# Bringing a vector to every partition: four transposes of a repeated column in place of a product of ones with a diagonal

## The chip, the cores and the metric

One Trainium2 chip, one core of it. The metric is the device time of one execution in microseconds (us), median of several runs. Everything is computed in FP32.

## The reference

Two layers over 4096 nodes with 512 features each; `adj` is a 4096 x 4096 matrix of weights.

```python
# layer 0: attention, its scores shifted twice by adj
q = x @ Wq.T + bq;  k = x @ Wk.T + bk;  v = x @ Wv.T + bv
a = q @ k.T / sqrt(512) + adj + adj
x = layernorm(x + softmax(a, axis=-1) @ v)
# layer 1: two graph convolutions
h = relu(adj @ (x @ W1) + b1)            # 128 features
x = layernorm(x + adj @ (h @ W2) + b2)
```

## The kernel before, in words

q and k are never formed. With M = Wq^T Wk, the scores are x M x^T plus terms that depend on one of the two nodes only: a column vector g made of Wq and bk, a vector ub made of Wk and bq, and a constant c0 made of bq and bk. The scores are halved and computed transposed, keys on the 128 partitions and queries along the free axis, because `adj` enters twice and the exponential is taken with scale 2. The products of the scores, of the softmax with x, and of the layers' matrices are done by Strassen's scheme with seven products in place of eight.

Queries are worked on in 8 groups g of 512 (`W`), keys in 8 blocks d of 512. One step of a group takes two of the seven products' places; a pair of 128-row key tiles is a unit. The order of all engines' work is written out by hand: the tile framework's scheduler is off, `at(unit, n, f)` puts a function at a place n of a unit, and a list `work` gives the TensorE work that is spread between the score products (products of the softmax with x for the group before, its output rows, the next layer's projection). Each engine carries out its own instructions in that order.

Five small vectors are needed in a form in which every partition holds the whole vector along its free axis (128 x 512), though they come as columns (128 x 4, entry r*128 + p at partition p, column r):

- bk and bq, at the very start. They are multiplied with the rows of Wq^T and Wk^T by VectorE (`times`) to make g and ub, and with each other to make c0.
- g, which VectorE multiplies with the rows of x (`row_parts`) to get each query's constant c.
- c of a group (8 times): `add_c0(g)` adds c0, `row_consts(g)` makes the tile CB[g], with which `begin_scores` fills a tile of scores on ScalarE (line 380). A DMA on GpSimd's queue then adds `adj` to it (line 385).
- m, the maximum of each query of a group (8 times): `turn_max(g)` turns the running maximum by four transposes (line 468), reduces it on VectorE (line 474) to a column per 128 queries; `spread_max(g)` makes MB[g], which VectorE subtracts from the scores (`shift`, line 484) ahead of the exponential.

Before the change each of these is done in two steps. `spread` (line 397, VectorE) multiplies an identity with the column, which gives four 128 x 128 diagonals in one 128 x 512 tile; the tile lies in the pool `sap` of eight buffers, which also holds the left operands of the score products ("sa"). `in_every_row` (line 408, TensorE) multiplies a matrix of ones, which is a 128 x 1 column read repeatedly, with the diagonals: each sum over the partitions has one term that isn't zero. ScalarE copies the result from PSUM (line 411). In the profile one such FP32 product shows as two matmul records. For c and m the two steps stand at different places of the schedule: m is reduced at place 5 of unit s1 and spread at place 1 of unit s1 + 1, c is completed at place 1 and spread at place 3 of a unit.

The stage at the start, before the loop: load bk and bq (ScalarE's queue), Wq^T and Wk^T in two halves each, then x^T and x (SP's queue); spread bk and bq; transpose Wq^T (tile `wq_t` into `wq_n`) and Wk^T by 16 transposes of 128 x 128 each (line 855), copied out in turn by ScalarE and VectorE; `times` for g; M by 16 products of 128 x 512 (tile psm, line 864), with g's broadcast after the second group of four; the first u = M^T x^T (psu, line 262), with the first group's c after its first four products.

PSUM is used in banks: four for the tag "o" (weights, u, softmax products), one each for "x" and "y" (scores), and one each for "m0" and "m1", which alternate for broadcasts, turns and output rows.

Of the kernel before, what the change touches and what calls it, by code (L numbers as in the profile page):

```python
# [11 lines left out]
F32 = mybir.dt.float32  # L12
AF = mybir.ActivationFunctionType
ALU = mybir.AluOpType
# [4 lines left out]
P = 128  # L19
# [5 lines left out]
def tile_graph_attention_then_gcn(  # L25
# [51 lines left out]
    nc = tc.nc  # L77
# [8 lines left out]
    PER = W // P  # L86
# [5 lines left out]
    const = ctx.enter_context(tc.tile_pool(name="const", bufs=1))  # L92
# [1 line left out]
    psum = ctx.enter_context(tc.tile_pool(name="psum", bufs=2, space=PSUM))  # L94

    ident = const.tile([P, P], F32, name="ident")
    ones = const.tile([P, 1], F32, name="ones")
    half_t = const.tile([P, 1], F32, name="half_t")
    bq_t = const.tile([P, ND], F32, name="bq_t")
    bk_t = const.tile([P, ND], F32, name="bk_t")  # L100
    b1_t = const.tile([P, 2], F32, name="b1_t")
    t_sb = const.tile([P, NT, H], F32, name="t_sb")
    c_sb = const.tile([P, NT], F32, name="c_sb")
# [18 lines left out]
    sap = att.enter_context(tc.tile_pool(name="sap", bufs=8, side="right"))  # L122
# [8 lines left out]
    g_t = mp.tile([P, D], F32, name="g_t")  # L131
# [4 lines left out]
    def bank(tag, name, bufs=1):  # L136
        return psum.tile([P, W], F32, tag=tag, name=name, bufs=bufs)
# [3 lines left out]
    def mbank(name):  # L141

        m_tags.append(m_tags.pop(0))
        return bank(m_tags[-1], name)
# [13 lines left out]
    UT, UO, XTS, SA, S, XN, CB, MB, MACC, LACC, O, OT, RL, XR, T = ({} for _ in range(15))  # L158


    def load_xts(b):
        XTS[b] = xtp.tile([P, ND, W], F32, tag="xt", name=f"xt{b}")
        nc.sync.dma_start(XTS[b], xT[:, ts(b, W)].rearrange("(c p) i -> p c i", p=P))
# [227 lines left out]
    def pair(g, q):  # L391
        return S[g, q // 2][:, :, q % 2]

    def spread(col, name):

        dg = sap.tile([P, PER, P], F32, tag="sa", name=f"diag{name}")
        nc.vector.tensor_tensor(
            dg,
            ident.unsqueeze(1).to_broadcast([P, PER, P]),
            col.unsqueeze(2).to_broadcast([P, PER, P]),  # L400
            ALU.mult,
        )
        T["diag", name] = dg

    def in_every_row(name, into):
        dg = T.pop(("diag", name))
        ps = mbank(f"bc{name}")
        nc.tensor.matmul(
            ps, ones.to_broadcast([P, P]), dg.rearrange("p r i -> p (r i)"), start=True, stop=True
        )  # L410
        nc.scalar.copy(into, ps)  # L411

    def load_rows(g):
# [3 lines left out]
    def row_parts(i, xr):  # L417

        product = t_sb[:, 24 : 24 + PER, :].rearrange("p a b -> p (a b)")
        nc.vector.scalar_tensor_tensor(  # L420
            product, xr, 1.0, g_t, ALU.mult, ALU.mult, accum_out=c_sb[:, i : i + 1]
        )

    def add_c0(g):
        c = c_sb[:, ts(g, PER)]
        nc.vector.tensor_scalar(c, c, c0_t, None, ALU.add)
        spread(c, f"c{g}")

    def row_consts(g):
        CB[g] = bcp.tile([P, W], F32, tag="cb", name=f"cb{g}")  # L430
        in_every_row(f"c{g}", CB[g])


    def qk(g, d, k, j):
# [30 lines left out]
    def turn(acc, name):  # L465
        ps = mbank(name)
        for r in range(PER):
            nc.tensor.transpose(ps[:, ts(r, P)], acc[:, ts(r, P)], ident)
        return ps.rearrange("p (r j) -> p r j", j=P)

    def turn_max(g):
        ps = turn(MACC[g], f"mt{g}")
        m = small.tile([P, PER], F32, tag="m", name=f"m{g}")
        nc.vector.tensor_reduce(m, ps, AX.X, ALU.max)
        spread(m, f"m{g}")

    def spread_max(g):
        MB[g] = bcp.tile([P, W], F32, tag="mb", name=f"mb{g}")
        in_every_row(f"m{g}", MB[g])


    def shift(g, q, h):
# [315 lines left out]
    with tc.tile_pool(name="wqk", bufs=1) as wp:  # L798
        wk_t = wp.tile([P, ND, D], F32, name="wk_t")
        wq_t = wp.tile([P, ND, D], F32, name="wq_t")  # L800
        wk_n = wp.tile([P, ND, D], F32, name="wk_n")
        wq_n = wp.tile([P, ND, D], F32, name="wq_n")
        bq_r = wp.tile([P, W], F32, name="bq_r")
        bk_r = wp.tile([P, W], F32, name="bk_r")
        g_c = wp.tile([P, ND], F32, name="g_c")

        nc.scalar.dma_start(bk_t, bk)
        nc.scalar.dma_start(bq_t, bq)
        for w_t, wT in ((wq_t, wqT), (wk_t, wkT)):
            for o in range(2):  # L810
                nc.sync.dma_start(
                    w_t[:, :, ts(o, D // 2)],
                    wT.rearrange("(c p) o -> p c o", p=P)[:, :, ts(o, D // 2)],
                )
        make_identity(nc, ident)
        nc.gpsimd.memset(ones, 1.0)
        nc.gpsimd.memset(half_t, -0.5)
        load_xts(0)
        rows0 = t_sb[:, : PER * PER, :].rearrange("p (r a) b -> p r (a b)", r=PER)
        nc.sync.dma_start(rows0, x[:W, :].rearrange("(r p) d -> p r d", p=P))  # L820
        load_xts(1)
        for i in range(4):
            nc.gpsimd.dma_start(
                b1_t[ts(i // 2, H // 2), i % 2 : i % 2 + 1], b1[ts(i % 2, H // 2), :]
            )
        def evict(n, out_, in_):
            if n % 2:
                nc.vector.tensor_copy(out_, in_)
            else:
                nc.scalar.copy(out_, in_)  # L830

        def times(w_t, b_r, into):

            product = t_sb[:, 24 : 24 + PER, :].rearrange("p a b -> p (a b)")
            for c in range(into.shape[1]):
                nc.vector.scalar_tensor_tensor(
                    product,
                    w_t[:, c, :],
                    HALF_SCALE,
                    b_r,  # L840
                    ALU.mult,
                    ALU.mult,
                    accum_out=into[:, c : c + 1],
                )

        for name, b_t, b_r in (("bk", bk_t, bk_r), ("bq", bq_t, bq_r)):
            spread(b_t, name)
            in_every_row(name, b_r)


        for w_t, w_n in ((wq_t, wq_n), (wk_t, wk_n)):
            for o in range(ND):
                ps = bank("o", f"psw{o}", 4)
                for c in range(ND):
                    nc.tensor.transpose(ps[:, ts(c, P)], w_t[:, c, ts(o, P)], ident)
                evict(o, w_n[:, o, :], ps)
        times(wq_t, bk_r, g_c)
        spread(g_c, "g")
        times(wk_t, bq_r, ub_t)

        for a in range(ND):
            ps = bank("o", f"psm{a}", 4)
            for o in range(ND):
                nc.tensor.matmul(  # L864
                    ps, wq_n[:, o, ts(a, P)], wk_n[:, o, :], start=o == 0, stop=o == ND - 1
                )
            evict(a, m_t[:, a, :], ps)
            if a == 1:
                in_every_row("g", g_t)
                times(bq_r.unsqueeze(1), bk_r, c0_t)  # L870
                for r in range(PER):
                    row_parts(r, rows0[:, r, :])
                add_c0(0)
# [5 lines left out]
    for f in first[:ND]:  # L879
        f()  # L880
    row_consts(0)
    begin_scores(0, 0)
    add_scores(0, 0)
# [243 lines left out]
    for g in range(NG):  # L1127
        s0 = g * NP
        s1 = s0 + NP
        if g:  # L1130
            for n, k in enumerate(ORDER):
                at(s0 - 2 + (2 * n + 1) // 7, (2 * n + 1) % 7, load_operand, g, k)
            at(s0 - 2 - (g == 1), 1, add_c0, g)
            at(s0 - 2 - (g == 1), 3, row_consts, g)
        for q in range(NP):
# [12 lines left out]
            at(s1 + unit, n2, sums, g, q)  # L1148
            at(s1 + unit, n2, px_t2, g, q)
        at(s1, 5, turn_max, g)  # L1150
        at(s1 + 1, 1, spread_max, g)
        if g < NG - 1:
            at(s1 + 13, 4, row_sums, g)
# [25 lines left out]
    for unit in range(last_unit):  # L1179
# [30 lines left out]
        for n in range(len(ORDER)):  # L1210
            run(unit, n)
            g, place = divmod(unit * len(ORDER) + n, NP * len(ORDER))
# [10 lines left out]
            while todo and owed > 0.2:  # L1223
                us, f = todo.pop(0)
# [7 lines left out]
    g = NG - 1  # L1232
# [106 lines left out]
    for n, (i0, cols, ld) in enumerate(parts):  # L1339
        acc = bank("o", f"acce{n}", 4)[:, :cols]  # L1340
        per = 2048 // cols
        for j in range(NT):
# [4 lines left out]
            if j % (2, 5, 10, 20)[n] == (1, 3, 4, 6)[n]:  # L1347
# [5 lines left out]
                start=j == 0,  # L1353
                stop=j == NT - 1,
# [49 lines left out]
```

## Time and profile before

| What | Value |
|---|---|
| median of 3 runs | 2315.63 us (2314.59 to 2316.66) |
| the profiled execution's own time | 2315.36 us |
| its span | 2313.5 us |
| TensorE matmul (PE) busy | 2285.4 us |
| TensorE weight load (PEld) busy | 1750.6 us |
| VectorE (DVE) busy | 1636.5 us |
| GpSimd (POOL) busy | 1010.3 us |
| ScalarE (ACT) busy | 403.9 us |
| granted TensorE clock, mean | 0.999 |

How to read it: PE is TensorE's matmuls, PEld its weight loads, which overlap them. Matmuls overlap one another in the records and their ends are modelled, so the time that one holds TensorE is read from start to start. Rows in order of time give the start and duration in us, the engine, the line of the kernel, the operation, and output and inputs by their names in the program; "x4" is a merged row of four instructions, and brackets hold the idle time of the engine before it and what ended that. A line of waits reads: who waited, on whom, us in total, times, the longest. "The chain of work that ended last" follows the time back from the last instruction through whatever released each step.

TensorE's operations that the change touches, from the profile of before:

| Operation | Count | Recorded ns of one |
|---|---|---|
| ones times diagonal of c, of m (line 408), records | 16 and 16 | 592 |
| the same for bk, for bq, records | 2 and 2 | 1061 to 1192 |
| the same for g, records | 2 | 592 |
| diagonals on VectorE (line 397) | 19 | 691 to 695 |
| transposes of the maximum (line 468) | 32 | 272 to 329 |
| transposes of Wq, Wk (line 855) | 32 | 272 to 421 |
| ScalarE's copies behind a broadcast (line 411) | 19 | 585 |

### The profile page before, as it was taken

How to read it: one execution, taken by the hardware profiler on the slowest of the kernel's cores; microseconds unless marked ns; L12 is line 12 of the kernel's file. 1: busy time of each engine (PE TensorE's matmuls, PEld its weight loads, DVE VectorE, ACT ScalarE, POOL GpSimd, SP SyncE). 2: the span in 40 equal slices, each digit the busy share in tenths (PEclk: the TensorE clock that was granted, in tenths of full speed). 3: DMA queues.
4: the chain of work that ended last, by engine and by line, in shares of the span. 5: the costliest groups of instructions: out<-in, count | busy, mean ns of one | idle time of the engine just before them, and what ended most of it. 6: DMA issues, size and time to landing. Idle time of an engine off the chain costs nothing.

```text
span 2313.5 us, 28534 instructions
## 1 busy us (share of the span) xinstructions
PE 2285.4 (99%) x10662; PEld 1750.6 (76%) x10662; DVE 1636.5 (71%) x2295; ACT 403.9 (17%) x445; POOL 1010.3 (44%) x1010
## 2 busy tenths in 40 slices
PE   9999999999999999999999999999999999999998
PEld 5888788888888888888888888888876743333456
DVE  4676776686667766866776787668657877888864
ACT  2212211231122112111311221122102000000012
POOL 2566553184237424731653284237429830001043
PEclk9999999999999999999999999999999999999999
DMA  6899786667757684877577577847654468899996
GB/s 173 268 302 306 229 246 200 177 186 210 229 141 217 187 241 112 227 197 210 149 224 215 152 217 195 233 132 218 192 195 149 161 237 312 334 346 375 352 381 223
DMA packets 278008, 523.30 MB, mean 226 GB/s; under 512 B 19376, under 2 KB 126640, under 8 KB 276976
## 3 DMA queue, kind: packets, MB, share of 16 engines
q1 hardware_dynamic: 229040, 406.12, 52.1%
q0 software_dynamic: 43296, 105.39, 20.6%
q10 hardware_dynamic: 5536, 9.97, 1.2%
q8 instruction: 85, 1.39, 0.2%
q14 instruction: 51, 0.42, 0.0%
HBM read 473.44 MB, written 46.40 MB: 225 GB/s over the span
## 4 chain that ended last, share of the span: by engine, by line
PE 94%; DVE 3%; POOL 2%; issue 1%; ACT 0%; DMA 0%; POOLq 0%; DVEq 0%; ACTq 0%
PE p L581 32%; PE X L441 19%; PE b L1049 15%; PE Y L441 14%; PE psu L234 3%; PE v L708 3%; PE acce L1349 2%; PE ops L1303 1%; PE tps L754 1%; PE psu L262 1%; PE x L656 1%; PE x1ps L745 1%; DVE s L531 1%; PE psm L864 1%; DVE s L454 1%
## 5 line engine op out<-in xcount | busy, mean ns | idle before, releaser
L581 PE MATMUL p<-s,xn 128*128 128x256 f32 x3584 | 895.9, 380 | 6.7 <-DVE s L531 2.7
L581 PEld LDWEIGHTS p<-s,xn 128*128 128x128 f32 x3584 | 676.9, 190 | 111.4 <-DVE s L531 6.2
L441 PE MATMUL X<-ut,sa 128*128 128x256 f32 x1984 | 513.3, 381 | 1.6 <-DVE s L454 1.6
L497 POOL TENSOR_TENSOR lacc<-lacc,s 128x512 f32<-128x512 f32 x240 | 344.4, 1435 | 203.2 <-ACT s L488 192.3
L441 PEld LDWEIGHTS X<-ut,sa 128*128 128x128 f32 x1984 | 370.4, 190 | 67.4 <-DVE s L454 15.3
L454 DVE TENSOR_TENSOR s<-X,s 128x512 f32<-128x512 f32 x256 | 176.4, 689 | 272.8 <-PE X L441 272.4
L441 PE MATMUL Y<-ut,sa 128*128 128x256 f32 x1408 | 360.7, 379 | 0.0
L441 PEld LDWEIGHTS Y<-ut,sa 128*128 128x128 f32 x1408 | 266.4, 190 | 39.6 <-issue 4.3
L488 ACT ACTIVATE s<-s 128x1024 f32<-128x1024 f32 x128 | 135.3, 1057 | 790.3 <-DVE s L484 790.3
L463 DVE TENSOR_TENSOR macc<-macc,s 128x512 f32<-128x512 f32 x240 | 253.7, 1057 | 1.2
L454 DVE TENSOR_TENSOR s<-Y,s 128x512 f32<-128x512 f32 x192 | 132.0, 688 | 151.6 <-PE Y L441 151.1
L385 POOL DMA_DIRECT2D s<-in_adjT_dram x64 | 84.4, 1319 | 353.8 <-ACT s L380 331.2
L484 DVE TENSOR_TENSOR s<-s,mb 128x512 f32<-128x512 f32 x256 | 231.1, 912 | 3.3 <-ACT mb L411 3.3
L554 DVE TENSOR_TENSOR ot<-p,ot 128x512 f32<-128x512 f32 x248 | 169.3, 682 | 31.6 <-PE p L581 31.4
L1016 DVE TENSOR_TENSOR tt<-ck 128x1024 f32<-128x1024 f32 x112 | 138.7, 1273 | 38.8 <-PE b L1049 33.5
L1049 PE MATMUL b<-tt,st 128*64 128x512 f32 (+1 forms) x768 | 156.1, 541 | 0.0
L531 DVE TENSOR_TENSOR s<-s 128x512 f32<-128x512 f32 x128 | 130.7, 1041 | 0.0
L524 POOL TENSOR_TENSOR s<-s 128x256 f32<-128x256 f32 x128 | 124.0, 969 | 0.6
L380 ACT COPY s<-cb 128x2048 f32<-128x2048 f32 x64 | 120.9, 1889 | 0.6
L1049 PEld LDWEIGHTS b<-tt,st 128*64 128x64 f32 x768 | 53.9, 137 | 87.8 <-issue 79.9
L525 POOL TENSOR_TENSOR s<-s 128x256 f32<-128x256 f32 x128 | 107.6, 841 | 10.0
L494 POOL TENSOR_TENSOR lacc<-s 128x512 f32<-128x512 f32 x8 | 10.6, 1321 | 200.2 <-ACT s L488 200.2
(192 smaller groups left out, 2132.6 us busy)
## 6 DMA issues: line engine op xcount, KB each, us to landing
ck<-in_adjT_dram SPq DMA_DIRECT2D x128, 1024.0 KB, 7.6
s<-in_adjT_dram POOLq DMA_DIRECT2D x64, 1024.0 KB, 11.6
sa<-s_d SPq DMA_DIRECT2D x224, 256.0 KB, 5.3
xn<-in_x_dram SPq DMA_DIRECT2D x192, 256.0 KB, 3.4
xn<-xs_d SPq DMA_DIRECT2D x96, 512.0 KB, 4.6
sa<-in_xT_dram SPq DMA_DIRECT2D x168, 256.0 KB, 4.4
xn<-xs_d SPq DMA_DIRECT2D x64, 256.0 KB, 3.8
ut<-u_d SPq DMA_DIRECT2D x49, 256.0 KB, 7.2
```

Source lines behind the costliest of these rows:

```text
L441: nc.tensor.matmul(T["X" if k in (1, 6, 5, 3) else "Y"][:, ts(j, HW)], SA[g, d, a][:, c, j, :], UT[g, b][:, c, :], start=k in (1, 2, 7) an ...
L454: nc.vector.tensor_tensor(ck, ps, ck, ALU.add)
L463: nc.vector.tensor_tensor(MACC[g], MACC[g], ck[:, h, :], ALU.max)
L484: nc.vector.tensor_tensor(ck, ck, MB[g], ALU.subtract)
L488: nc.scalar.activation(ck, ck, AF.Exp, scale=2.0)
L497: nc.gpsimd.tensor_tensor(LACC[g], LACC[g], ck[:, h, :], ALU.add)
L524: nc.gpsimd.tensor_tensor(b12, b12, b11, ALU.subtract)
L531: nc.vector.tensor_tensor(b, b, t2, ALU.subtract)
L554: nc.vector.tensor_tensor(to, ps, to, ALU.add)
L581: nc.tensor.matmul(T["PX" if k in (1, 6, 5, 3) else "PY"][:, ts(f, HW)], XN[n][:, q - a, ts(f, P)], quarters(g, q)[{1: 0, 2: 2, 6: 1, 7: 0 ...
L1016: nc.vector.tensor_tensor(t[:, :2], v[:, :, 1], v[:, 0], ALU.subtract)
L1049: nc.tensor.matmul(BK[n][k][ts(half, HH)], lhs, right(u, i, half, b), start=q == 0, stop=q == NP - 1,)
```

## The change

`spread` and the column of ones go. `in_every_row` is given the column itself: for each of its four parts it reads the 128 x 1 column repeatedly as a 128 x 128 matrix and transposes that with the identity, so that every row of the result is the column. One broadcast is then four transposes of 128 x 128 into one PSUM bank, and ScalarE's copy as before. c, m and g are spread at the same places of the schedule as before; the diagonals that VectorE made at the places before them are gone. At the start, bk is spread ahead of Wq's transposes as before, and bq now behind them, ahead of Wk's.

```diff
-    def spread(col, name):
-
-        dg = sap.tile([P, PER, P], F32, tag="sa", name=f"diag{name}")
-        nc.vector.tensor_tensor(
-            dg,
-            ident.unsqueeze(1).to_broadcast([P, PER, P]),
-            col.unsqueeze(2).to_broadcast([P, PER, P]),
-            ALU.mult,
-        )
-        T["diag", name] = dg
-
-    def in_every_row(name, into):
-        dg = T.pop(("diag", name))
+    def in_every_row(name, col, into):
+
         ps = mbank(f"bc{name}")
-        nc.tensor.matmul(
-            ps, ones.to_broadcast([P, P]), dg.rearrange("p r i -> p (r i)"), start=True, stop=True
-        )
+        for r in range(PER):
+            nc.tensor.transpose(ps[:, ts(r, P)], col[:, r : r + 1].to_broadcast([P, P]), ident)
         nc.scalar.copy(into, ps)
...
         nc.vector.tensor_scalar(c, c, c0_t, None, ALU.add)
-        spread(c, f"c{g}")
...
-        in_every_row(f"c{g}", CB[g])
+        in_every_row(f"c{g}", c_sb[:, ts(g, PER)], CB[g])
...
-        spread(m, f"m{g}")
+        T["m", g] = m
...
-        in_every_row(f"m{g}", MB[g])
+        in_every_row(f"m{g}", T.pop(("m", g)), MB[g])
...
-        for name, b_t, b_r in (("bk", bk_t, bk_r), ("bq", bq_t, bq_r)):
-            spread(b_t, name)
-            in_every_row(name, b_r)
-
-
-        for w_t, w_n in ((wq_t, wq_n), (wk_t, wk_n)):
+
+        for w_t, w_n, name, b_t, b_r in (
+            (wq_t, wq_n, "bk", bk_t, bk_r), (wk_t, wk_n, "bq", bq_t, bq_r)
+        ):
+            in_every_row(name, b_t, b_r)
             for o in range(ND):
                 ps = bank("o", f"psw{o}", 4)
                 for c in range(ND):
                     nc.tensor.transpose(ps[:, ts(c, P)], w_t[:, c, ts(o, P)], ident)
                 evict(o, w_n[:, o, :], ps)
         times(wq_t, bk_r, g_c)
-        spread(g_c, "g")
         times(wk_t, bq_r, ub_t)
...
-                in_every_row("g", g_t)
+                in_every_row("g", g_c, g_t)
```

Also gone are the tile `ones` and the memset that filled it on GpSimd.

## Prediction

> **What bounds the kernel now.** I read the page first: busy shares, the slices, the chain of work that ended last. Then TensorE's waits over the whole span, then the first 45 us in order of time, and last the neighbourhood of single broadcasts in the middle of the kernel.
>
> ```profile
> span 2313.5 us, 28534 instructions
> PE 2285.4 (99%) x10662; PEld 1750.6 (76%) x10662; DVE 1636.5 (71%) x2295; ACT 403.9 (17%) x445; POOL 1010.3 (44%) x1010
> ...
> PE 94%; DVE 3%; POOL 2%; issue 1%; ACT 0%; DMA 0%; POOLq 0%; DVEq 0%; ACTq 0%
> ```
>
> TensorE is busy for 99% of the span and holds 94% of the chain. So what TensorE itself gains counts nearly in full, and what VectorE alone gains counts only where TensorE waits for it. Over 2313.5 us the waits of TensorE's matmuls come to some 16 us besides the first one; these are the longest groups:
>
> ```profile
> PE bcbk L408 <- DVE diagbk L397: 5.1, 1, 5.1
> PE X L441 <- DVE s L454: 3.3, 5, 0.9
> PE p L581 <- DVE s L531: 2.7, 6, 0.7
> ```
>
> No broadcast but the very first (bk's) is waited for. Two kinds of row give the price of the change. The first two rows below are around one of c's broadcasts, the next three around an existing group of four transposes (line 468 turns the row sums in the same way):
>
> ```profile
> 404.82 1.02 PE L408 MATMUL bcc<-diagc,ones 128*128 128x512 f32 x2
> 405.68 1.03 PE L441 MATMUL Y<-ut,sa 128*128 128x256 f32 x4
> ```
>
> ```profile
> 392.54 1.03 PE L581 MATMUL p<-s,xn 128*128 128x256 f32 x4
> 393.40 0.60 PE L468 MATMUL l<-ident,lacc 128*128 128x128 f32 x4
> 393.84 0.38 PE L441 MATMUL Y<-ut,sa 128*128 128x256 f32 x1
> ```
>
> Read the starts, not the durations, since matmuls overlap: the product holds TensorE for 405.68 - 404.82 = 0.86 us, four transposes for 393.84 - 393.40 = 0.44 us. Other groups of four take 0.43 (434.36 to 434.79).
>
> The start of the kernel is a case of its own:
>
> ```profile
> 4.23 0.69 DVE L397 TENSOR_TENSOR diagbk<-ident,bk_t 128x512 f32<-128x512 f32 x1 [4.23 <-DMA bk_t<-in_bk_dram]
> ...
> 5.07 2.05 PE L408 MATMUL bcbk<-diagbk,ones 128*128 128x512 f32 x2 [5.07 <-DVE diagbk L397]
> ...
> 6.91 1.97 PE L408 MATMUL bcbq<-diagbq,ones 128*128 128x512 f32 x2
> ...
> 8.67 2.29 PE L855 MATMUL psw<-ident,wq_t 128*128 128x128 f32 x16
> ...
> 10.80 1.91 PE L855 MATMUL psw<-ident,wk_t 128*128 128x128 f32 x16
> ...
> 12.54 7.03 PE L864 MATMUL psm<-wk_n,wq_n 128*128 128x512 f32 x16
> ```
>
> The first two products are 1.84 and 1.76 us apart instead of 0.86: TensorE runs at half pace. The first transposes of Wq still start 0.21 us apart (8.67, 8.88, 9.10), then from about 9.3 they come every 0.11. So the pace doubled some 4.2 us after the first product.
>
> **What the Trainium skill says.** "TensorE: Matmul & The Clock Gate", Part 1 (the HAM clock gate): TensorE starts at half clock and gets the full one after about 3.4 us of sustained activity, judged in a free-running window. The trace agrees in kind: 4.2 us from 5.07. The same page, Part 4 (PE-mode transpose): for transposes the full clock "doesn't engage", they don't count as busy in the same way. The trace doesn't settle it: the pace doubled after 3.6 us of products, and it held through the transposes from 9.3 to 12.5, 3.2 us, less than one such window. Its Terms table calls transpose mode four times faster for FP32; here 512 columns by transposes are only twice as fast (0.43 against 0.86), and I use the trace. "VectorE: DVE Perf Modes", the section on the TRN2 errata, gives (N+151)/0.96 ns for an FP32 tensor_tensor, 691 ns at 512; the diagonals measure 691 to 695.
>
> **The change, part by part.**
>
> (1) Nineteen diagonals on VectorE (8 for c, 8 for m, and g, bk, bq) go: 19 x 0.69 = 13.1 us. Only bk's and bq's are waited for, and they are counted in (3). The others I take at nothing: after m's reduction there are some 3 us before the product that needs it. Bound: TensorE's waits for VectorE within 12 us of a diagonal (0.20 at 205 us, 0.78 at 245 us) could shrink, at most 1 us; no extra wait arises, since the transposes need m or c itself, which is there 0.7 us before its diagonal.
>
> (2) Fifteen broadcasts in the loop (c of groups 1 to 7, m of groups 0 to 7): each 0.86 becomes 0.435, saving 0.425. All of them stand in an unbroken row of TensorE work, so 15 x 0.425 = 6.4 us. Then g's and the first c's, at 19.4 and 30.6 us: 2 x 0.425 = 0.85. Sum 7.2 us. The new operand is a column read 128 times over as weights. No transpose in the trace does that; the products already load such a repeated column (the ones), at 190 ns a load, the same as line 581's ordinary ones. So I take no surcharge. From below no gain is likely; from above, a surcharge of half a transpose (0.05 us x 68) would take 3.7 us away. ScalarE's copy behind each broadcast is unchanged and comes 0.43 us earlier.
>
> (3) The start. Before, the first product of Wq and Wk (psm) starts at 12.54. After, bk's transposes can start when bk has landed, about 4.25 instead of 5.07. Ten groups of four transposes then lie ahead of psm (bk, four of Wq, bq, four of Wk), with no product among them. Wq's halves land at about 0.73 + 4.1 = 4.8 and 1.2 + 5.3 = 6.5, Wk's at 1.75 + 7.0 = 8.75 and 2.3 + 8.1 = 10.4, from the issues and their times to landing. If transposes don't raise the clock, the ten groups take 10 x 4 x 0.215 = 8.6 us, and psm starts at 12.85, 0.3 later than before, no transfer being late. Then psm's first stretch runs at half pace: at the 4.2 us seen before, half of that is lost, 2.1 us. With the page's window it is 3.4 to 6.8 us, so 1.7 to 3.4 lost. Sum of the start: +2.4 (2.0 to 3.7). If transposes do raise it, four groups are done by 8.5, and then Wk's second half at 10.4 is late: psm starts at about 11.3, saving 1.2.
>
> (4) Moves. bq's transposes go behind Wq's, bq's copy on ScalarE behind Wq's copies; bq's broadcast is first read by VectorE at 16.9, long after. On VectorE the column sums wait for nothing new. SP and GpSimd keep their order of work; a memset of 0.1 us goes. The diagonals no longer take buffers of the pool that holds the left operands, so some loads start earlier; TensorE never waits for those loads before, so nothing.
>
> Sum with the slow start: -7.2 + 2.4 = -4.8. The profiled execution took 2315.36 (span 2313.5), 0.27 below the median of 2315.63; on the median that is 2310.8.
>
> **The rivals.**
> A, the forecast: transposes don't raise the clock. 2310.8, from 2310.4 to 2312.1 by the length of the slow stretch. For it: the skill's sentence. Against: nothing in the trace.
> B: they do. 2315.6 - 7.2 - 1.2 = 2307.2, down to 2306.3 with VectorE's relief. For it: the pace held through 3.2 us of transposes.
> C: the loop's gain is waited out, because VectorE's reads pace each step. Then only the start and the 0.85 remain: 2315.6 + 2.4 - 0.85 = 2317.2 (2313.6 with B's start). For it: VectorE at 71%, and waits of 0.8 us at some boundaries. Against: TensorE's records stand without gaps around nearly every broadcast, and VectorE's reads start when TensorE ends, so they move with it.
> D, slower: TensorE stays at half clock well into the first stage. Place: from psm on. Price: half of the time that it lasts, beside the 7.2 gained and 0.3 lost. It is even at 13.8 us and slower by over 0.2% from 23 us on; up to the first scores at 42 us (29 us) it would be 2315.6 - 7.2 + 0.3 + 14.6 = 2323.3. Against: before, 4.2 us sufficed.
>
> **How the numbers follow.** A 0.56, B 0.32, C 0.08, D 0.04. A measurement tells some 0.2%, 4.6 us, from no change, so faster means below 2311.0. A falls on both sides of that, slightly oftener in "same" (its long slow stretches); B is faster, C the same, D slower: faster 0.59, same 0.37, slower 0.04. The range reaches from B's low end to A's high end and the surcharge's beginning: 2306.4 to 2312.7, leaving out C, D and little else.
>
> **What would show it.** Step 2: starts 0.43 us apart from a broadcast's first transpose to the next work; 0.86 would mean a surcharge. Step 3: the pace of Wq's and Wk's transposes (0.215 or 0.11 apart), the start of psm (12.85 or 11.3), and the pace of psm's first rows (0.86 or 0.43). Step 1: the waits for VectorE near 205 and 245 us. The prediction is wrong if psm's start and pace are those of B, if the gaps that are saved return as waits for VectorE, or if loads of the left operands become late.

## The result and the profile after

| | median us | range | runs |
|---|---|---|---|
| before | 2314.85 | 2314.30 to 2316.66 | 6 |
| after | 2306.36 | 2305.53 to 2307.39 | 6 |

The ratio is 0.996, with a 95% interval of 0.995 to 0.9971: faster by 8.5 us, where 4.8 was forecast, and just below the range, which began at 2306.4. The profiled execution took 2306.20 us.

From the page of the changed kernel, the span, the busy times and the engines' shares of the chain:

```profile
span 2304.1 us, 28523 instructions
...
PE 2277.0 (99%) x10700; PEld 1752.6 (76%) x10700; DVE 1624.9 (71%) x2276; ACT 404.0 (18%) x445; POOL 1011.0 (44%) x1009
...
PE 92%; DVE 3%; POOL 3%; issue 1%; DMA 0%; ACT 0%; POOLq 0%; SPq 0%; DVEq 0%; ACTq 0%
```

TensorE's busy time falls by 8.4 us and the span by 9.4; VectorE loses 11.6 us of work. TensorE still bounds the kernel. Its longest waits are much the same as before:

```profile
PE bcbk L397 <- DMA bk_t<-in_bk_dram: 4.1, 1, 4.1
PE X L427 <- DVE s L440: 3.7, 5, 0.9
PE p L567 <- DVE s L522: 3.3, 3, 1.7
```

The first line is new in one thing: TensorE starts when bk lands, not when VectorE has made a diagonal of it. The third is line 536 of the kernel before, which came fourth there with 2.6 us in two waits. In the middle of the kernel, one of c's broadcasts and what follows it:

```profile
402.02 0.60 PE L397 MATMUL bcc<-ident,c_sb 128*128 128x128 f32 x4
402.46 1.03 PE L427 MATMUL Y<-ut,sa 128*128 128x256 f32 x4
```

From start to start 0.44 us, as priced (0.86 before). Read repeatedly, the column costs nothing extra: its weight loads take 137 ns, those of ordinary transposes 139 to 142. The start of the kernel, TensorE alone:

```profile
4.05 1.09 PE L397 MATMUL bcbk<-ident,bk_t 128*128 128x128 f32 x4 [4.05 <-DMA bk_t<-in_bk_dram]
4.93 3.62 PE L839 MATMUL psw<-ident,wq_t 128*128 128x128 f32 x16
8.35 0.93 PE L397 MATMUL bcbq<-ident,bq_t 128*128 128x128 f32 x4
9.11 1.04 PE L839 MATMUL psw<-ident,wk_t 128*128 128x128 f32 x8
10.41 1.06 PE L839 MATMUL psw<-ident,wk_t 128*128 128x128 f32 x8 [0.26 <-ACT wk_n L815]
11.31 7.03 PE L847 MATMUL psm<-wk_n,wq_n 128*128 128x512 f32 x16
```

Wq's 16 transposes take 3.42 us from start to start, 0.214 each: half pace. bq's four take 0.76, so the pace doubles with the last of them, at about 9.0. Wk's first eight start at 9.11 and would end at 9.98, at 0.109 each. No product has run by then, so the clock needs none to rise. There is a short gap ahead of 10.41. The row names ScalarE's copy of Wk, which ended at the same moment; in start_only and diag_kept below the same gap, ending at 10.41 and 10.40, names the transfer of Wk's second half, and that is what I take. psm starts at 11.31 and runs at full pace (16 records in the same 7.03 us as before).

Where the 9.4 us between the two spans came from, read from starts at the same places:

| Place | before | after | gain so far |
|---|---|---|---|
| psm's first row | 12.54 | 11.31 | 1.23 |
| c's first broadcast (g's lies ahead) | 30.57 | 28.92 | 1.65 |
| c's second | 198.10 | 196.03 | 2.07 |
| c's third (m's first lies ahead) | 404.82 | 402.02 | 2.80 |
| m's second | 439.97 | 436.76 | 3.21 |
| m's seventh | 1517.30 | 1510.24 | 7.06 |
| m's eighth | 1726.11 | 1718.17 | 7.94 |
| end | 2313.5 | 2304.1 | 9.4 |

Of the sixteen steps from one broadcast to the next, from g's to m's eighth, twelve are 0.41 to 0.43. The other four are 0.06, 0.66, 0.06 and 0.87: they lose 0.72 and win 0.69 against that, so they cancel. In the profiled executions of before, after and the eight experiments, the stretch from m's eighth broadcast to the end lies between 585.4 and 587.4 us; before's is the longest of all, after's 585.9. So about 1 us of the 9.4 lies in the spread of single executions. The medians give 8.5.

### The profile page after: what moved, and what is told of

It reads as the page before. It is cut to its first block, busy times and chain, and to the rows that moved or that the text cites. A ratio compares the mean times of both kernels' runs of the same rounds, so it can differ in the third digit from the quotient of the medians.

```text
span 2304.1 us, 28523 instructions
## 1 busy us (share of the span) xinstructions
PE 2277.0 (99%) x10700; PEld 1752.6 (76%) x10700; DVE 1624.9 (71%) x2276; ACT 404.0 (18%) x445; POOL 1011.0 (44%) x1009
## 4 chain that ended last, share of the span: by engine, by line
PE 92%; DVE 3%; POOL 3%; issue 1%; DMA 0%; ACT 0%; POOLq 0%; SPq 0%; DVEq 0%; ACTq 0%
PE p L567 31%; PE X L427 18%; PE b L1032 15%; PE Y L427 14%; PE psu L233 3%; PE v L694 3%; PE acce L1332 2%; PE ops L1286 1%; PE psu L261 1%; PE tps L740 1%; POOL lacc L483 1%; PE x L642 1%; PE x1ps L731 1%; PE psm L847 1%; DVE s L517 1%
```

## The experiments

Theory T: transposes raise and hold TensorE's clock as products do, so the gain is the shorter broadcasts (17 x 0.425 = 7.2 us) plus a start that ends with Wk's transfer (1.2 us). Rivals: S, that transposes don't count for the clock; K, that the clock rises at a time after the kernel's start, whatever TensorE does; R, that VectorE's relief gives part of the gain; M, that the move of bq gives the start's gain.

The medians, in microseconds; each line stands beside runs of the kernel before on the same chip (2315.36 for the first four, 2315.64 for the next three, 2315.46 for the last).

| Run | median | range | ratio to before (95%) |
|---|---|---|---|
| start_only | 2312.93 | 2312.46 to 2314.18 | 0.999 (0.9982 to 0.9998) |
| loop_only | 2308.20 | 2307.40 to 2308.83 | 0.997 (0.9958 to 0.9981) |
| bq_first | 2307.56 | 2306.85 to 2308.18 | 0.9967 (0.9954 to 0.9979) |
| diag_kept | 2306.50 | 2305.87 to 2307.24 | 0.9963 (0.995 to 0.9975) |
| hold_96 | 2317.43 | 2317.05 to 2318.92 | 1.0009 (1.0 to 1.0017) |
| early_12 | 2306.39 | 2306.00 to 2307.03 | 0.9961 (0.9948 to 0.9975) |
| early_12_x_late | 2306.74 | 2306.29 to 2307.20 | 0.9963 (0.995 to 0.9975) |
| early_12_wk_act | 2314.90 | 2313.44 to 2316.50 | 0.9996 (0.9987 to 1.0004) |

### start_only and loop_only: the two halves of the change

start_only is the kernel before with this (and g likewise); c and m stay with diagonals. `by_transposes` is the changed kernel's `in_every_row`, put in beside the old one:

```diff
-        for name, b_t, b_r in (("bk", bk_t, bk_r), ("bq", bq_t, bq_r)):
-            spread(b_t, name)
-            in_every_row(name, b_r)
-        for w_t, w_n in ((wq_t, wq_n), (wk_t, wk_n)):
+        for w_t, w_n, name, b_t, b_r in (
+            (wq_t, wq_n, "bk", bk_t, bk_r), (wk_t, wk_n, "bq", bq_t, bq_r)
+        ):
+            by_transposes(name, b_t, b_r)
```

> Only the start is changed: bk, bq (behind Wq's transposes) and g are spread by transposes, c and m still by products with diagonals. Theory T (transposes raise TensorE's clock as products do, and the start ends with Wk's second half): psm starts at 11.3 instead of 12.5, and g's broadcast saves 0.43, so 1.65 us below the kernel before, 2313.2. Rival S (transposes don't count for the clock, what the changed kernel gained at the start came from elsewhere): psm slow at its beginning, 2 us above the kernel before, 2317. Rival R (the changed kernel gained more than the sum of the shorter broadcasts, from VectorE being free): the same as T here, since no diagonal is gone in the loop.

loop_only is the kernel before with the other half:

```diff
-        spread(c, f"c{g}")
-        in_every_row(f"c{g}", CB[g])
+        by_transposes(f"c{g}", c_sb[:, ts(g, PER)], CB[g])
-        spread(m, f"m{g}")
-        in_every_row(f"m{g}", MB[g])
+        by_transposes(f"m{g}", T.pop(("m", g)), MB[g])
```

> Only c and m are spread by transposes (16 broadcasts); bk, bq and g still by products with diagonals, ahead of everything. Theory T: 16 x 0.425 = 6.8 us below the kernel before, 2308.0, and together with the start's gain this makes the whole. Rival C (the loop's gain is waited out at VectorE's reads): 2313 or more. Rival R (VectorE's relief adds to it): 2307 or less.

start_only gained 2.4 us and loop_only 7.2, against 1.65 and 6.8 by T. S, which wanted the start 2 us slower than before, is out, and so is C, the prediction's rival by which the loop's gain is waited out. The two halves together make 9.6; the whole made 8.5 in its own runs and 8.9 beside these (diag_kept below); the intervals, some 2 to 3 us to either side, cover that. In start_only's profile psm starts at 11.31, to the hundredth as in the changed kernel, right behind Wk's second half:

```profile
10.41 1.06 PE L859 MATMUL psw<-ident,wk_t 128*128 128x128 f32 x8 [0.64 <-DMA wk_t<-in_wkT_dram]
11.31 7.03 PE L867 MATMUL psm<-wk_n,wq_n 128*128 128x512 f32 x16
```

loop_only has the start of the kernel before, yet its psm starts at 13.21 and not at 12.54:

```profile
13.21 7.03 PE L869 MATMUL psm<-wk_n,wq_n 128*128 128x512 f32 x16
```

The pace doubled only at 11.0 there, and at 9.4 in the profile of before. So the start's gain isn't one number; what moves it stands under early_12.

### diag_kept: what VectorE's relief is worth

The changed kernel, in which VectorE makes the 16 diagonals of c and m all the same; nobody reads them. `dead` does what `spread` did before.

```diff
         nc.vector.tensor_scalar(c, c, c0_t, None, ALU.add)
+        dead(c, f"c{g}")
...
+        dead(m, f"m{g}")
         T["m", g] = m
```

> The changed kernel, but VectorE still makes the 16 diagonals of c and m at their old places, into buffers of the same pool, and nobody reads them: 16 x 0.69 = 11 us of VectorE's time more. Theory T (VectorE's time there was worth nothing): 2306.4, within 0.4 of the changed kernel. Rival R (VectorE's relief gave what exceeds the sum of the shorter broadcasts): 2307.3 or more.

2306.50 against 2306.36: the 16 diagonals, 11 us of VectorE's time, were worth nothing. R is out, and step 1 stands. The gain of the loop is TensorE's own.

### hold_96: do transposes hold the clock?

The changed kernel with 96 transposes more ahead of psm, into a bank that nobody reads; nothing is left out.

```diff
+        idle = bank("x", "idle")
+        for n in range(96):
+            nc.tensor.transpose(idle[:, ts(n % PER, P)], ident, ident)
         times(wq_t, bk_r, g_c)
```

> The changed kernel with 96 more transposes of the identity between Wk's transposes and psm, into a bank that nobody reads (work added, nothing left out). With bk's, bq's and the weights' that makes a stretch of 136 transposes without one product. Theory T (transposes raise and hold the clock): all 96 at 0.109 us, 10.4 us in all, psm at full pace from its first row (0.43 between rows): 10.4 above the changed kernel, 2316.8. Rival S (transposes don't count as busy): [...]later transposes come 0.215 apart, and psm's first rows 0.86 apart: 2320 or more.

TensorE from its first work on:

```profile
4.24 1.08 PE L397 MATMUL bcbk<-ident,bk_t 128*128 128x128 f32 x4 [4.24 <-DMA bk_t<-in_bk_dram]
5.12 3.62 PE L839 MATMUL psw<-ident,wq_t 128*128 128x128 f32 x16
8.53 0.80 PE L397 MATMUL bcbq<-ident,bq_t 128*128 128x128 f32 x4
...
11.29 10.64 PE L843 MATMUL idle<-ident 128*128 128x128 f32 x96
21.77 2.74 PE L850 MATMUL psm<-wk_n,wq_n 128*128 128x512 f32 x6
```

The 96 take 21.77 - 11.29 = 10.48 us, 0.109 each, to the last. From the doubling at about 8.9 to psm at 21.77 TensorE did nothing but transposes for 12.8 us, and psm still began at full pace: the first six records fill 2.74 us, 0.43 apart. The median rose by 11.1 over the changed kernel, 10.4 expected. S is out on both counts, raising and holding.

### early_12: activity or time?

```diff
+        idle = bank("x", "idle")
+        for n in range(12):
+            nc.tensor.transpose(idle[:, ts(n % PER, P)], ident, ident)
         for w_t, w_n, name, b_t, b_r in (
```

> The changed kernel with 12 transposes of the identity put ahead of bk's, from when the identity is there (about 1.4 us); nobody reads them. They end at 1.4 + 12 x 0.215 = 4.0, when bk lands. Theory T (activity of any kind raises the clock): the pace doubles 4.2 to 4.7 us after 1.4, at 5.6 to 6.1, early among Wq's transposes; the start's end is still set by Wk's second half at 10.4, so psm at 11.25 and 2306.3, no gain. Rival K (the clock rises at a time after the kernel's start, not after TensorE's first work): the pace doubles at about 8.8 as in the changed kernel. Rival S: not before psm.

TensorE in its profile, up to psm:

```profile
1.35 2.82 PE L834 MATMUL idle<-ident 128*128 128x128 f32 x12 [1.35 <-POOL half_t L802]
4.26 0.95 PE L397 MATMUL bcbk<-ident,bk_t 128*128 128x128 f32 x4
5.05 1.06 PE L843 MATMUL psw<-ident,wq_t 128*128 128x128 f32 x8
6.50 1.09 PE L843 MATMUL psw<-ident,wq_t 128*128 128x128 f32 x8 [0.38 <-DMA wq_t<-in_wqT_dram]
7.42 0.60 PE L397 MATMUL bcbq<-ident,bq_t 128*128 128x128 f32 x4
8.98 1.06 PE L843 MATMUL psw<-ident,wk_t 128*128 128x128 f32 x8 [0.96 <-DMA wk_t<-in_wkT_dram]
10.51 1.06 PE L843 MATMUL psw<-ident,wk_t 128*128 128x128 f32 x8 [0.46 <-DMA wk_t<-in_wkT_dram]
11.41 1.02 PE L851 MATMUL psm<-wk_n,wq_n 128*128 128x512 f32 x2
```

Eight transposes in 1.06 us, the same as the fast ones at 8.98, show the full pace from 5.05 on: at most 3.7 us after TensorE's first work at 1.35 (T had 4.2 to 4.7), and some 4 us earlier than in the changed kernel. Now TensorE waits before each half of a matrix, and psm starts at 11.41 all the same: transfers set the start's end. The time (2306.39) is that of the changed kernel, as T said.

One execution would not be enough to put K out, since the moment of the rise scatters. The traces' record of the granted clock has it for all ten profiles, within 0.1 us of where the starts show the pace doubling (early_12_x_late and early_12_wk_act follow below):

| Run | first work | rise | after first work | busy in the 3.41 us before the rise | in the 3.41 us before those |
|---|---|---|---|---|---|
| before | 5.07 | 9.44 | 4.4 | 3.41 | 0.95 |
| after | 4.05 | 9.01 | 5.0 | 3.41 | 1.53 |
| start_only | 4.10 | 7.00 | 2.9 | 2.90 | 0 |
| diag_kept | 4.07 | 6.97 | 2.9 | 2.90 | 0 |
| hold_96 | 4.24 | 8.93 | 4.7 | 3.41 | 1.27 |
| loop_only | 4.89 | 11.02 | 6.1 | 3.41 | 2.71 |
| bq_first | 4.10 | 11.66 | 7.6 | 3.41 | 2.81 |
| early_12 | 1.35 | 4.92 | 3.6 | 3.33 | 0.15 |
| early_12_x_late | 1.35 | 6.75 | 5.4 | 3.37 | 1.99 |
| early_12_wk_act | 1.35 | 4.35 | 3.0 | 3.00 | 0 |

With the 12 transposes ahead the rise comes at 4.4 to 6.8, without them at 7.0 to 11.7: K is out. The last two columns, TensorE's busy time, show why it scatters. In each record the next change of the clock comes a whole number of 3.413 us after the rise: 2 of them in early_12_wk_act, 671 to 675 (at the kernel's end) in the others. So the clock is set window by window, every 3.413 us, and the executions start at different places in a window. It rises at the end of the first window in which TensorE was busy for 2.90 us or more; windows with up to 2.81 did not count. Transposes fill a window as products do.

### bq_first: the move alone

```diff
-        for w_t, w_n, name, b_t, b_r in (
-            (wq_t, wq_n, "bk", bk_t, bk_r), (wk_t, wk_n, "bq", bq_t, bq_r)
-        ):
-            in_every_row(name, b_t, b_r)
+        in_every_row("bk", bk_t, bk_r)
+        in_every_row("bq", bq_t, bq_r)
+        for w_t, w_n in ((wq_t, wq_n), (wk_t, wk_n)):
```

> The changed kernel with bq's transposes ahead of Wq's again, right behind bk's. Theory T: bq lands at about 6.0, so TensorE stands idle for some 1.1 us between bk's and bq's transposes, with everything behind it 1.1 later; the clock rises about 4.5 us after the first transpose or later, since there is a gap. Wk's second half at 10.4 then still sets psm's start or nearly so: psm at 11.3 to 12.0, 2306.4 to 2307.1. Rival M (the move is most of the start's gain): psm at 12.4 or later, 2307.5 or more.

TensorE in its profile, up to psm:

```profile
4.10 1.09 PE L397 MATMUL bcbk<-ident,bk_t 128*128 128x128 f32 x4 [4.10 <-DMA bk_t<-in_bk_dram]
5.79 1.12 PE L397 MATMUL bcbq<-ident,bq_t 128*128 128x128 f32 x4 [0.60 <-DMA bq_t<-in_bq_dram]
6.70 3.62 PE L838 MATMUL psw<-ident,wq_t 128*128 128x128 f32 x16
10.12 2.67 PE L838 MATMUL psw<-ident,wk_t 128*128 128x128 f32 x16
12.62 1.88 PE L846 MATMUL psm<-wk_n,wq_n 128*128 128x512 f32 x4
```

It took 2307.56, 1.06 above diag_kept, which stood beside it and took the changed kernel's time. M fits the median and this psm better than my expectation from T, but the two kernels' ranges overlap, and the profiled execution is the slowest of the five (2308.18). TensorE waits for bq (it lands 1.7 us after bk) while Wq, which is there, stands behind. The window with this gap was busy for 2.81 us and did not count, so the clock rose only at 11.66.

An estimate from these rows: from 6.70 to Wk's second half at 10.4 there is room for the 24 transposes that lie ahead of it if the pace doubles by 8.9, 4.8 us after the first work. The same count for the changed kernel (28 transposes from 4.93) gives 9.9, 5.8 us after it. So what the move gives is 1 us more in which a late rise stays hidden behind Wk's transfer. What that is worth in an execution hangs on where its windows lie; about 1 us of the medians is all that was measured.

### early_12_x_late and early_12_wk_act: can the start's end be moved?

The first is early_12 with the loads of x^T and x behind a small store that waits for bk's broadcast; the second is early_12 with Wk's halves on ScalarE's queue.

```diff
+            if name == "bk":
+                nc.sync.dma_start(held, bk_r[:, :PER])
+                load_xts(0)
...
-                nc.sync.dma_start(
+                (nc.sync if w_t is wq_t else nc.scalar).dma_start(
                     w_t[:, :, ts(o, D // 2)],
```

> As early_12, and the loads of x^T and x are held back on SP's queue by a small store that waits for bk's broadcast on ScalarE, so that Wk's halves have the DMA engines to themselves. Theory T (the start then ends with Wk's second half alone): Wk's second half lands near 8.5 to 9.0 instead of 10.4, psm starts at 9.5 to 10, 1.3 to 1.8 below the changed kernel, 2304.6 to 2305.1. Rival L (the halves are held by their own issue and latency, not by the loads behind them): Wk lands as before, 2306.3. Rival X (x^T or x is now late): waits at psu or at the first dot products of x, above 2306.4.

> As early_12 (the clock is raised before Wk lands), and Wk's two halves are issued on ScalarE's queue behind bk and bq instead of SP's behind Wq. Between 5 and 7 us the DMA engines moved only some 180 GB/s in the changed kernel. Theory Q (one queue's transfers stand behind one another, and a second queue fills that dip): Wk's second half lands at 9.4 to 9.9 instead of 10.4, psm starts at 10.3 to 10.8, 0.5 to 1.0 below early_12, 2305.4 to 2305.9. Rival E (the DMA engines or memory set it, whatever the queue): 2306.4; Wq may land later, by what Wk takes from it.

Neither helped. With x held back (issued at 6.36 instead of 2.86), Wk's halves still took 7.0 and 7.9 us from issue to landing (6.9 and 8.0 in the changed kernel) and psm started at 11.27: the loads behind Wk were not what kept it. The packets of the changed kernel say the same: between 6.4 and 9 us none of x's, which hold 2 KB, moved, while those of 1 KB (Wk's) did. L's sign came true, though what sets those 8 us is open: between 5 and 7 us the DMA engines move only 185 to 290 GB/s, against 340 to 390 from 7 on.

On ScalarE's queue Wk moved beside x instead of ahead of it, which none of my theories had, and the time was 2314.90, 8.5 us above early_12:

```profile
7.51 0.60 PE L397 MATMUL bcbq<-ident,bq_t 128*128 128x128 f32 x4
12.26 1.94 PE L843 MATMUL psw<-ident,wk_t 128*128 128x128 f32 x8 [4.15 <-DMA wk_t<-in_wkT_dram]
16.25 1.94 PE L843 MATMUL psw<-ident,wk_t 128*128 128x128 f32 x8 [2.05 <-DMA wk_t<-in_wkT_dram]
```

SP, which no longer issues Wk, issues x^T and x 1.1 us earlier, and the two queues take turns: from 9 to 14 us ScalarE's moved 663 packets with 0.66 MB and SP's 666 with 1.33 MB. So Wk, whose packets are half as long, got a third of the bytes, and its halves land at about 12.2 and 16.2 instead of 8.9 and 10.5. The run also shows the clock's other direction: after 4.15 us without work Wk's eight transposes take 1.94 us (0.21 each) where they took 1.06, and psm's first 16 records 8.75 where they took 7.03. The record has the fall at 11.18, at the end of a window with 0.34 us of TensorE's work. So an idle TensorE loses the pace, and a transposing one doesn't.

## Why the prediction was wrong, point by point

- **Step 1**, VectorE's diagonals at nothing: right. diag_kept puts 11 us of them back at no cost. Of the waits named as a sign, the one near 205 us grew from 0.20 to 0.55 (see C below), and the one near 245 stayed (0.78 and 0.79).
- **Step 2**, 0.425 us for each of 17 broadcasts and no surcharge for the repeated column: right. A product held TensorE for 0.86 us and four transposes for 0.44 at all 17, and loop_only gained 7.2 where 6.8 was worked out.
- **Step 3** failed, at "if transposes don't raise the clock". The branch taken put the start at +2.4 us: psm at 12.85, and 2.1 us lost at half pace. Measured: psm at 11.31 and no row of it at half pace, -1.2. The other branch had 11.3 and -1.2. With it, 7.2 + 1.2 = 8.4 us, and 8.5 was measured. The mechanism of rival B was right, and its odds too low. That the sums agree to 0.1 us is luck: the interval is 2.4 us to either side, and the start of before, from which the 1.2 is counted, ended at 12.54 in one profile and at 13.21 in loop_only's.
- Why the odds were wrong: I let a sentence of the Trainium skill ("TensorE: Matmul & The Clock Gate", Part 4) outweigh the trace of before, in which the full pace held through 3.2 us of transposes. I called that undecided, since it is less than the window that the page gives, and wrote "nothing in the trace" against the forecast. hold_96 stretched it to 12.8 us: the measurement decides, and for these FP32 transposes of 128 x 128 the sentence doesn't hold. The page's Part 1, on the other hand, agrees: a rise after activity, a fall after idle time, and the free-running window, which shows in the traces with 3.413 us (early_12). The prediction's own reading of it, 3.4 to 6.8 us, is nearly what was found (2.9 to 6.1 us, and 7.6 with a gap), but it was put to products alone.
- **The low end** of the range was B's from the median of three runs; that median was 0.8 us above the one of six. From 2314.85, B's sum gives 2306.45.
- **Step 4**, moves at nothing: right for SP's and GpSimd's order, but "bq's transposes go behind Wq's" was taken as harmless, while the median is about 1 us higher without it (bq_first, ranges overlapping). It keeps TensorE from waiting for bq and so leaves Wk's transfer more of the clock's late rise to hide. I had counted it inside B's 1.2 without seeing that part of it hangs on the move.
- **Rivals C and D**: no sign. Two places lost most of one broadcast's gain. Near 514 us 0.34 is lost, where TensorE newly waits 0.17 for a transfer (tile xn). The other is near 203 us: at 196 us the changed kernel is 2.07 ahead, c's second broadcast should make that 2.50 by 203, and it is 2.14 (205.37 against 203.23). The wait for VectorE there grew from 0.20 to 0.55. The row of VectorE that grew, in order of time in the kernel before:

```profile
202.36 0.68 DVE L420 SCALAR_TENSOR_TENSOR t_sb<-t_sb,g_t 128x512 f32<-128x512 f32 x1
202.39 1.78 POOL L219 TENSOR_TENSOR uo<-uo,b 128x512 f32<-128x512 f32 x1
```

and in the changed kernel:

```profile
199.07 1.27 POOL L218 TENSOR_TENSOR uo<-uo 128x512 f32<-128x512 f32 x1
...
199.87 1.02 DVE L407 SCALAR_TENSOR_TENSOR t_sb<-t_sb,g_t 128x512 f32<-128x512 f32 x1
```

Before, VectorE's instruction started just ahead of GpSimd's and took its 0.68. After, GpSimd's was under way until 200.34, and VectorE's ends 0.55 after that. The skill's page "SBUF — State Buffer", section "SBUF: two separate sides", says that a VectorE operation with two inputs in SBUF and a GpSimd operation that reads SBUF share a port pair, which whoever starts first holds to its instruction's end; the rows agree. VectorE's row takes 1.02 in every run that spreads c by transposes, diag_kept with its diagonals among them, and 0.68 in start_only, where c is spread as before. It cost 0.35 us once. That the ports are the cause is inferred from the rows, since no run took the GpSimd row away.

## What to carry to other kernels

Where TensorE is the bound, transposes of the repeated column bring a column to every partition at half the cost of the product with a diagonal: in FP32 0.44 us for 512 entries against 0.86, with no diagonal to make. Ways that leave TensorE out were not tried. Look at the start of a kernel as its own stage, with its own bound (here a transfer landing at 10.4 us), and put work that waits for a late small transfer behind work whose data are there. When a rule about the clock decides a forecast's sign or size, look for the stretch of the trace that already tests it, and give the rule no more weight than that stretch.

## What the runs showed of the hardware

- Transposes alone raise TensorE's clock and hold it (a rise 4.7 us after the first one in hold_96, then 12.8 us held); 4.15 us of idling lose it.
- The clock changes only at the ends of windows of 3.413 us, and the executions start at different places in one. A window with 2.90 us or more of TensorE's busy time raised it, one with 2.81 did not; so the rise came 2.9 to 7.6 us after the first work, and the same start ended 0.67 us apart in two profiles.
- The column of the granted clock shows 1.00 in the first microseconds although the pace there is half (0.214 against 0.109 us a transpose), since the record's first entry is the rise: at a kernel's start the pace must be read from the starts of instructions. After the fall in early_12_wk_act it does show 0.50.
- Transfers of one queue stood in line (x's packets behind Wk's), those of two queues took turns packet by packet (663 and 666 from 9 to 14 us): on a queue of its own Wk's second half landed 5.7 us later, since x's longer packets moved beside it.
